# A two-layer graph attention kernel: sums of h behind the first maxima, W's rows on ScalarE's queue, VectorE kept in order at the joint, end stores on other queues

## The chip, the cores and the metric

The kernel runs on one core of one Trainium2 chip. The metric is the device time of one execution in microseconds (us). A profiled execution also gives a span, from its first to its last recorded event, and the clock that was granted to TensorE at each moment.

## What is computed

Two layers are applied to 2708 nodes with 1024 features in float32, over a sparse adjacency matrix. Cut to what matters:

```python
def layer0(x, adj, Wf, bf, Wg, bg, W, bW):
    f, g = x @ Wf + bf, x @ Wg + bg
    e = relu(f @ g.T)
    att = softmax(where(adj > 0, e, NEG), axis=1)
    return att @ (x @ W + bW)

def layer1(x, adj, W, a1, a2):
    h = x @ W
    e = leaky_relu(h @ a1 + (h @ a2).T, 0.2)
    att = softmax(where(adj > 0, e, NEG), axis=1)
    return relu(att @ h)

x = x + layer0(maximum(layernorm(x), 0), ...)
x = x + layer1(maximum(layernorm(x), 0), ...)
```

## The kernel before

**Tiling.** The nodes are cut into five panels of columns (NP = 5; 576, 576, 532, 512 and 512 wide) and ten pairs of row tiles (NQ = 10), with two small tiles left over (MONO and TINY). Every large matrix product is done in seven half-size products, M1 to M7, with sums of blocks before and after (the Strassen-Winograd scheme). The right-hand and left-hand sums of blocks are made by VectorE. Those of h, the normalized rows, lie in DRAM (`hg_d`, seven slots of which `sums_h` fills four, M3 and M5 to M7, from the two that it loads twice: M1 and M2 hold the plain blocks), and are loaded as tiles called `hc` when a product needs them.

**Stages of layer 0**, panel by panel in the loop at L1697: `scores` makes the score tiles S of a panel and accumulates their maxima in `acc`; `project_q(p + 1)` makes the queries of the next panel, and meanwhile, through hooks after its products, `take_max` (M1) turns the maxima by TensorE (`mx_ps`, L849, in `column_max`) and `take_softmax` (M2) makes the exponentials and their sums `sm`; `aggregate` (L885) multiplies S by h in products gx, gy, gz, gv through `accumulate` (L647), whose matmuls are at L661; `inverse_sums` (L858) sums `sm` over partitions with two matmuls into `sum_ps` (L864) and takes reciprocals on VectorE into `rr`; `scale` (L975) multiplies the result gT by them on GpSimd; `project` (L1203, matmuls L1267) multiplies by W and adds the residual x. In panel 0 `aggregate` runs its products in the order M1, M2, M4, M5, M6, M3, M7, in the other panels M1, M5, M2, M6, M3, M7, M4. In the middle of M7, `into_m15` (L933) computes the left-over rows' part (four groups `gw`, L931) and VectorE adds them in.

**The joint.** After the loop, `project(0, 4)` finishes the last panel of layer 0. For each finished row tile, `rows_done` (L1523) normalizes it into `h_last` (ScalarE), takes the dot products with two vectors (`dots(1)`, which the first maxima of layer 1 need, and `dots(0)`, deferred with `put`), and `raise_max` updates `mx`. The last tile calls `shifts1` (L1505), in which `column_max` again turns the maxima (`mx_ps`), and then the column shift m is spread over the partitions by transposes (`sp_ps`, L253) in `weights1` (L1738), which subtracts the spread `mb` from prepared score tiles. Layer 1 then aggregates as layer 0 does and ends with `finish1` (its `go` at L1802), which applies relu, adds the residual and stores to the output.

**W's rows.** `prepare_W` (L1305) loads the rows of the two W (tiles `w_rows`), takes dot products of layer 1's rows with a1 and a2 on VectorE, and makes and stores the sums of W's blocks (`wt_d`).

**What sets the order.** The Tile framework moves instructions within an engine's queue by its own scheduler, unless an instruction is kept in program order; the class `InOrder` does this for the engines named in `nc.hold` (L34 to 54). Loads go through SyncE's queue and are kept in program order (L137); stores go through GpSimd's queue (L141). [...] The tiles `hc`, `hr`, `w_rows`, `hl`, `md`, `As` and `w` share one pool of 12 buffers (`strm`), so a load waits until an earlier tile's last reader is done. Side work is put into a queue `later` (`put`, L198) with a cost in microseconds and, where given, a fetch, which `one` (L201) issues `ahead[0]` items ahead, and a condition `ready`; `behind(us)` (L211) takes items off it between matmuls of a stage, up to the credit of that stage, and `sums_until(n)` and `flush` take them off at once.

Of the kernel before, what the change touches and what calls it, by code (L numbers as in the profile page):

```python
# [12 lines left out]
OP = mybir.AluOpType  # L13
# [5 lines left out]
P = 128  # L19
# [38 lines left out]
def kernel(  # L58
# [152 lines left out]
    def behind(us, psum_free=False):  # L211
# [3 lines left out]
        while spare[0] and not later and lazy and credit[0] > 0:  # L215
            credit[0] -= one(lazy)

    def flush():
        while later:
            one()  # L220
# [141 lines left out]
    def sums_h():  # L362

        def fetch(q, two):
            i, j = group_of[q]
            for m in (M1, M2):
                two.append(stream("hr", (P, 2, W)))
                load(two[-1], hg_d[i][:, m:m + 2, j])

        def first(q, two):  # L370
            (a0, a1), (b0, b1) = ((t[:, 0], t[:, 1]) for t in two)
            add(b1, a1, b1)
            sub(a1, a0, a1)

        def second(q, two):
            (a0, a1), (b0, b1) = ((t[:, 0], t[:, 1]) for t in two)
            sub(a0, b1, a0)
            sub(b0, b0, a0)
            i, j = group_of[q]
            store(hg_d[i][:, M6:M7 + 1, j], two[0])  # L380
            store(hg_d[i][:, M3, j], b0)
            store(hg_d[i][:, M5, j], b1)
            summed[0] += 1
        for q in range(NQ):
            two = []
            put(1.4, lambda q=q, two=two: first(q, two), lambda q=q, two=two: fetch(q, two))
            put(1.4, lambda q=q, two=two: second(q, two))

    BY_QUARTERS = (M1, M5, M2, M6, M7, M3, M4)
    made_quarters = {}  # L390
# [132 lines left out]
            one()  # L523


    def load_rows(w, c, name):
        t = stream(name)
        load(t, w[c * P:(c + 1) * P, :])
        return t

    wgT, wfT, M, m_left = [None, None], {}, {}, {}

# [352 lines left out]
    def aggregate(l, p, S, sm, then={}, rate=3.0):  # L885
# [89 lines left out]
        def scale():  # L975
            for e, s, k in ((0, slice(0, w), w), (1, hi, h)):
                nc.gpsimd.tensor_tensor(of(e, s), of(e, s), by(s, k), OP.mult)  # L977

        accumulate(left, right, NQ, h, order, then, evict, "g",
                   {**prepare, M3: lambda: inverse.append(inverse_sums(p, sm)), M7: scale}, rate=rate,  # L980
                   by_k=True, more={M2: lambda ps: left_over(ps, 0, lo), M3: lambda ps: left_over(ps, 0, hi),
                                    M4: lambda ps: left_over(ps, 1, lo),
                                    (M7, NQ // 2): lambda: (into_m15(), then.get((M7, "middle"), lambda: None)())})
        nc.vector.tensor_tensor(of(1, lo), of(1, lo), by(lo, h), OP.mult)
        return [t.rearrange("p (c i) -> p c i", c=NH) for t in G]

# [318 lines left out]
    def prepare_W():  # L1305
        ab, rows = [], {}

        def fetch(l, k):
            if l == 1 and not ab:
                for k2, a in enumerate((a1, a2)):  # L1310
                    row_to_all(a, wab[k2])
                ab.extend(halves(t) for t in wab)
            rows[l, k] = [load_rows(w_in[l], c, "w_rows") for c in (k, k + NH)]

        def go(l, k):
            two = rows.pop((l, k))
            if l == 1:
                for i, c in enumerate((k, k + NH)):
                    for j in range(2):
                        dot(wa[:, j, c:c + 1], halves(two[i]), ab[j])  # L1320
            right_of_W(l, k, *two)

        for l in range(2):
            for k in range(NH):
                put(2.7 if l == 0 else 8.0, lambda l=l, k=k: go(l, k), lambda l=l, k=k: fetch(l, k))
# [197 lines left out]
    def rows_done(t, xt):  # L1523
# [14 lines left out]
        if panel_of[t] == NP - 1:  # L1538
            done_rows[t] = row_halves("h_last")
            normalize(xt, done_rows[t])  # L1540
            if whole and q == NQ - 1:
                tc.keep_in_program_order(nc.scalar.activation(stats.tile([P, 1], FP, name="warm"), eps, AF.Exp))
            raise_it = lambda: raise_max(0, q, k, first_mask[t][:, :width[0]])
            if not whole:
                dots(1)
                raise_later.append(raise_it)
                put(1.6, lambda: dots(0))
            else:
                raise_later.pop()()
                dots(1)  # L1550
                raise_it()
                put(1.6, lambda: dots(0))
                rest = []
                make = lambda: rest.append(pair_h(q, *(done_rows[s] for s in pairs[q])))
                if q == NQ - 1:
                    got["zm"] = shifts1(0, make)
                else:
                    make()
                rest[0]()
                put_max(1, q)  # L1560
                if q == NQ - 1:
                    for m in BY_QUARTERS:
                        put_quarters(m, q // 2, later)
                    for p in range(2, NP):
                        for s in (NQ - 2, NQ - 1):
                            put_max(p, s, lazy)
            return
# [123 lines left out]
    def take_max(p):  # L1691
        got["m"] = column_max(p, got["acc"])
# [6 lines left out]
    for p in range(NP):  # L1699
# [3 lines left out]
        S = got["S"]  # L1703
        hooks = {M1: lambda p=p: take_max(p), M2: lambda p=p: take_softmax(p)}
        if p == 0:
            hooks[M1] = lambda: (take_max(0), sums_until(3))
            sums_h()
        if p + 1 < NP:
            B = project_q(p + 1, hooks)
        else:  # L1710
# [1 line left out]
            project(0, p - 1, G.pop(p - 1), finish0(p - 1), hooks)  # L1712
            nc.hold = ()
            scores_before()
        then = {M4: lambda: sums_until(NQ), M5: prepare_W} if p == 0 else {}
        ahead[0] = 1 if p == 0 else 2
        if p == NP - 2:
            then[M2] = lambda: first_masks(NP - 1, 0)
# [11 lines left out]
        if p < NP - 2:  # L1730
            project(0, p, G.pop(p), finish0(p), {M1: lambda p=p: first_masks(p + 1, 0),
                                                 M5: lambda p=p: first_masks(p + 1, 1),
                                                 M7: lambda p=p: first_masks(p + 1, 2)})
    flush()
    project(0, NP - 1, G.pop(NP - 1), finish0(NP - 1), by_pair=True, rate=0.0)


    def weights1(p, z, m, shift):  # L1738
# [6 lines left out]
            spread(vb1, columns_of(p, m))  # L1745
        if p == 0:
            mb = slot("mb")
            spread(mb, columns_of(p, shift))
        else:
            spreads()  # L1750
        S = [None] * NT
# [3 lines left out]
        def go(i, mk):  # L1755
            if i < len(order):
                q, k = order[i]
                n, t = P, units[q][k]
                if p == 0 and t in before:
                    S[t] = before.pop(t)  # L1760
                    s = S[t][:n, :w]
                    sub(s, s, mb[:n, :w])
                else:
                    if p == 0 and not spreaded:
                        spreads()
                        spreaded.append(True)
                    S[t] = slot("P")
                    s = S[t][:n, :w]
                    nc.scalar.activation(s, vb1[:n, :w], AF.Identity, bias=f2s[:n, t:t + 1])
                    nc.vector.scalar_tensor_tensor(s, ub[:n, :w], f[1][:n, t:t + 1], s, op0=OP.add, op1=OP.max)  # L1770
                    add(s, s, mk[0][:n, :w])
                nc.scalar.activation(s, s, AF.Exp)
            if i >= LAG:
                q, k = order[i - LAG]
                total(p, sm, S[units[q][k]], once(q, k), i == LAG)
            exps[0] += 1
# [10 lines left out]
    def finish1(p):  # L1787
# [12 lines left out]
                    load(xs[t][e], x1_d[t][:, e * W:(e + 1) * W])  # L1800

        def go(t, e, c):  # L1802
            o = slot("o")[:, :c.shape[1]]
            nc.scalar.activation(o, c, AF.Relu)
            add(xs[t][e], xs[t][e], o)
            if t == TINY:
                for ps, to in by_quarters(out, places[t][0][1], e):
                    store(to, xs[t][e][ps])
# [58 lines left out]
```

## Time and profile before

| | before |
|---|---|
| median of three runs | 3084.98 us (3083.76 to 3087.26) |
| profiled execution, its own time | 3084.88 us |
| span of the profiled execution | 3083.0 us |
| mean granted TensorE clock | 0.991 of full |
| instructions | 41611 |
| TensorE (PE) busy | 3000.3 us, 97% |
| VectorE (DVE) busy | 2069.9 us, 67% |
| GpSimd (POOL) busy | 504.1 us, 16% |
| ScalarE (ACT) busy | 460.9 us, 15% |
| data moved by DMA | 766.79 MB, mean 249 GB/s |

How to read the lines below. In a timeline a line has the start in us, the length in us, the engine (SPq is SyncE's queue of DMA issues), the line of the kernel, the operation, output and inputs, the shape, how many, and in brackets the idle time before it and what ended it. Line 45 is the helper through which VectorE and ScalarE operations are recorded, so there the tile names tell what it is. In the table of waits a line names the engine and its waiting instruction, after the arrow who released it, and then the total, the count and the longest wait in us. In the table of windows a line has the window, its length, the busy time of TensorE's matmuls, its weight loads, VectorE, ScalarE and GpSimd with the number of instructions, then the granted clock, the DMA share and GB/s.

### The profile page before, as it was taken

Reading aid. Unit: us, or ns where it says so; the run is one execution under the profiler, and the core shown is the slowest. Engines: PE = TensorE matmul, PEld = TensorE weight load, DVE = VectorE, ACT = ScalarE, POOL = GpSimd, SP = SyncE. Lnnn points to the kernel's source line nnn. Section 1 sums busy time; section 2 is a strip of 40 time slices with the busy share of each in tenths; the row PEclk is TensorE's granted clock in tenths of the full one; section 3 lists DMA queues with packets and bytes.
Section 4 is the critical chain, followed back from the end, with each engine's and each line's share of the span. In section 5 each row is a group of like instructions: output and inputs, shape, how many; then the busy total and the mean of one; then the engine's idle time right before and its main releaser. Section 6 shows DMA issues by size and latency. Waiting matters only on the chain.

```text
span 3083.0 us, 41611 instructions
## 1 busy us (share of the span) xinstructions
PE 3000.3 (97%) x14630; PEld 2299.3 (75%) x14630; DVE 2069.9 (67%) x4615; ACT 460.9 (15%) x815; POOL 504.1 (16%) x786
## 2 busy tenths in 40 slices
PE   8998999899999999999999999998999999999998
PEld 4576777657877588885888887784767959879695
DVE  5766692776651596716966276867878768887853
ACT  3420020000110101101011001302222131212200
POOL 1421101310011110214102011131202010020202
PEclk9999999999999999999999999998999999999999
DMA  6989967998565796758967588689767768888797
GB/s 226 300 257 272 291 244 255 307 281 226 178 234 154 216 261 223 246 156 239 274 212 249 161 237 272 225 292 327 242 207 254 270 205 293 292 267 295 265 296 248
DMA packets 447808, 766.79 MB, mean 249 GB/s; under 512 B 175488, under 2 KB 262304, under 8 KB 447568
## 3 DMA queue, kind: packets, MB, share of 16 engines
q1 hardware_dynamic: 392624, 598.30, 62.0%
q0 software_dynamic: 54976, 165.83, 16.5%
q8 instruction: 116, 1.90, 0.2%
q14 instruction: 92, 0.75, 0.1%
HBM read 630.04 MB, written 138.11 MB: 249 GB/s over the span
## 4 chain that ended last, share of the span: by engine, by line
PE 74%; DVE 11%; issue 7%; DMA 5%; POOL 1%; SPq 1%; ACT 1%; POOLq 0%; DVEq 0%; ACTq 0%
PE sz L1378 6%; PE gx L661 6%; PE gy L661 6%; PE gz L661 5%; PE gz L1067 5%; PE sx L1378 4%; PE pz L1267 4%; PE px L1267 4%; PE sy L1378 4%; PE py L1267 3%; PE gy L1067 3%; PE gx L1067 3%; PE gv L661 3%; PE M_ps L574 3%; PE qz L661 2%
## 5 line engine op out<-in xcount | busy, mean ns | idle before, releaser
L1378 PE MATMUL sz<-B,As 128*128 128x288 f32 (+2 forms) x1200 | 296.1, 396 | 10.2 <-DVE st L45 8.1
L1378 PEld LDWEIGHTS sz<-B,As 128*128 128x128 f32 x1200 | 229.8, 192 | 61.0 <-DVE st L45 12.1
L1378 PE MATMUL sx<-B,As 128*128 128x288 f32 (+2 forms) x800 | 201.7, 395 | 8.2 <-DMA As<-hs_d 6.2
L1378 PE MATMUL sy<-B,As 128*128 128x288 f32 (+2 forms) x800 | 199.2, 392 | 0.5 <-DMA As<-hs_d 0.5
L661 PE MATMUL gz<-Sa,hc 128*128 128x288 f32 (+2 forms) x800 | 188.3, 396 | 5.9 <-DMA hc<-hg_d 5.9
L1378 PEld LDWEIGHTS sx<-B,As 128*128 128x128 f32 x800 | 152.3, 191 | 42.7 <-issue 5.0
L661 PEld LDWEIGHTS gz<-Sa,hc 128*128 128x128 f32 x800 | 153.3, 192 | 39.2 <-DMA hc<-hg_d 6.3
L1378 PEld LDWEIGHTS sy<-B,As 128*128 128x128 f32 x800 | 152.1, 190 | 31.4 <-issue 0.9
L1067 PE MATMUL gz<-quarter,hc 128*128 128x128 f32 (+2 forms) x1344 | 168.8, 279 | 3.8 <-DVE gT L45 3.7
L143 POOL DMA_DIRECT2D out_dram<-x_res x180 | 88.8, 500 | 482.2 <-DVE x_res L45 471.1
L1067 PEld LDWEIGHTS gz<-quarter,hc 128*128 128x128 f32 x1344 | 160.6, 191 | 5.1 <-DVE gT L45 4.5
L1267 PE MATMUL px<-w,gT 128*128 128x512 f32 x320 | 141.2, 593 | 1.5 <-ACT pt L45 1.5
L1267 PE MATMUL py<-w,ps 128*128 128x512 f32 x320 | 142.2, 593 | 0.0
L1267 PE MATMUL pz<-w,ps 128*128 128x512 f32 x320 | 142.1, 594 | 0.0
L143 POOL DMA_DIRECT2D mk_d<-mask x55 | 35.9, 653 | 530.6 <-DVE mask L45 524.2
L1267 PEld LDWEIGHTS pz<-w,ps 128*128 128x128 f32 x320 | 60.2, 190 | 76.2 <-issue 71.0
L1267 PEld LDWEIGHTS py<-w,ps 128*128 128x128 f32 x320 | 60.5, 190 | 75.1 <-issue 72.7
L1267 PEld LDWEIGHTS px<-w,gT 128*128 128x128 f32 x320 | 60.1, 190 | 72.9 <-issue 67.8
L574 PE MATMUL M_ps<-wgT,wfT 128*128 128x512 f32 x256 | 111.8, 593 | 1.6 <-ACT hsT L45 1.6
L661 PE MATMUL gy<-T,hc 128*128 128x288 f32 (+2 forms) x480 | 111.6, 394 | 0.0
L977 POOL TENSOR_TENSOR gT<-gT,rr 128x2304 f32<-128x2304 f32 (+5 forms) x12 | 44.4, 3698 | 375.6 <-DVE rr L45 172.4
L661 PEld LDWEIGHTS gy<-T,hc 128*128 128x128 f32 x480 | 91.2, 190 | 19.5
(379 smaller groups left out, 5809.6 us busy)
## 6 DMA issues: line engine op xcount, KB each, us to landing
hc<-hg_d SPq DMA_DIRECT2D x175, 512.0 KB
As<-hs_d SPq DMA_DIRECT2D x150, 512.0 KB
hc<-hr_d SPq DMA_DIRECT2D x119, 512.0 KB
hc<-hs_d SPq DMA_DIRECT2D x112, 512.0 KB
w<-wt_d SPq DMA_DIRECT2D x96, 512.0 KB
w<-in_L_gnn_W_dram SPq DMA_DIRECT2D x72, 512.0 KB
md<-md_d SPq DMA_DIRECT2D x56, 512.0 KB
adj_i<-in_adj_dram SPq DMA_DIRECT2D x200, 128.0 KB
```

What stands on the lines that cost most here:

```text
L143: nc.gpsimd.dma_start(a, b)
L574: nc.tensor.matmul(ps, wfT[a][c // NH][:, c % NH, :], wgT[b][c], start=(c == 0), stop=(c == NC - 1))
L661: nc.tensor.matmul(ps[d], left(m, k, d), right(m, k), start=(start and k == 0), stop=(k == K - 1), skip_group_check=True)
L977: nc.gpsimd.tensor_tensor(of(e, s), of(e, s), by(s, k), OP.mult)
L1067: nc.tensor.matmul(ps[:, d], lhs[:, d * P:(d + 1) * P], inner_right(m, n, k), start=(start and k == 0 and d == 0), stop=(k == NK - 1), ski ...
L1267: nc.tensor.matmul(ps, left[i][m][:, k, :], w_[k], start=(start and k == 0), stop=(k == NH - 1), skip_group_check=True)
L1378: nc.tensor.matmul(ps[:n, :h], lefts[q][:, i % 2, c, :n], B[m][c // 2][:, c % 2, :h], start=(start and c == 0), stop=(c == NH - 1), skip_g ...
```

## The change

Six edits:

1. A helper `held` runs a function with VectorE kept in program order.
2. `sums_h`: the fetches of the first two pairs are issued at once, ahead of the loads of the next panel's queries; every item is held in order, and may be taken only after `take_max` has run (`"m" in got`). The hook after M1 of panel 0 no longer calls `sums_until(3)` and runs `take_max` held.
3. `load_rows` gets an argument for the queue. W's rows are loaded by ScalarE's queue, in program order, and `prepare_W` is called after M2 of panel 0's aggregate and no longer after M5, so the first rows are asked for in the third product, M4.
4. `inverse_sums` is called in the middle of M7, ahead of `into_m15`, and no longer at the end of M3, in all five panels of layer 0 and in panel 0 of layer 1.
5. At the joint `project(0, 4)`, `dots(0)`, the spread of `mb` and the first three subtractions of `weights1` are held in order on VectorE.
6. `finish1` of the last panel: relu and addition become one VectorE instruction in place of one on ScalarE and one on VectorE. The last two row tiles are stored by SyncE's and ScalarE's queues in turn, 16 stores, and no longer by GpSimd's.

```diff
+    def held(f, *a):
+        was, nc.hold = nc.hold, ("vector",)
+        r = f(*a)
+        nc.hold = was
+        return r
...
         for q in range(NQ):
             two = []
-            put(1.4, lambda q=q, two=two: first(q, two), lambda q=q, two=two: fetch(q, two))
-            put(1.4, lambda q=q, two=two: second(q, two))
+            if q < 2:
+                fetch(q, two)
+            put(1.4, lambda q=q, two=two: held(first, q, two), None if q < 2 else lambda q=q, two=two: fetch(q, two),
+                ready=lambda: "m" in got)
+            put(1.4, lambda q=q, two=two: held(second, q, two), ready=lambda: "m" in got)
...
-    def load_rows(w, c, name):
+    def load_rows(w, c, name, by=load):
         t = stream(name)
-        load(t, w[c * P:(c + 1) * P, :])
+        by(t, w[c * P:(c + 1) * P, :])
         return t
+
+    def by_scalar(o, i):
+        tc.keep_in_program_order(nc.scalar.dma_start(o, i))
...
         accumulate(left, right, NQ, h, order, then, evict, "g",
-                   {**prepare, M3: lambda: inverse.append(inverse_sums(p, sm)), M7: scale}, rate=rate,
+                   {**prepare, M7: scale}, rate=rate,
                    by_k=True, more={M2: lambda ps: left_over(ps, 0, lo), M3: lambda ps: left_over(ps, 0, hi),
                                     M4: lambda ps: left_over(ps, 1, lo),
-                                    (M7, NQ // 2): lambda: (into_m15(), then.get((M7, "middle"), lambda: None)())})
+                                    (M7, NQ // 2): lambda: (inverse.append(inverse_sums(p, sm)), into_m15(), then.get((M7, "middle"), lambda: None)())})
...
-            rows[l, k] = [load_rows(w_in[l], c, "w_rows") for c in (k, k + NH)]
+            rows[l, k] = [load_rows(w_in[l], c, "w_rows", by_scalar) for c in (k, k + NH)]
...
-                put(1.6, lambda: dots(0))
+                put(1.6, lambda: held(dots, 0))
...
-            hooks[M1] = lambda: (take_max(0), sums_until(3))
+            hooks[M1] = lambda: held(take_max, 0)
             sums_h()
...
-        then = {M4: lambda: sums_until(NQ), M5: prepare_W} if p == 0 else {}
+        then = {M2: prepare_W, M4: lambda: sums_until(NQ)} if p == 0 else {}
...
     flush()
+    nc.hold = ("vector",)
     project(0, NP - 1, G.pop(NP - 1), finish0(NP - 1), by_pair=True, rate=0.0)
+    nc.hold = ()
...
-            spread(mb, columns_of(p, shift))
+            held(spread, mb, columns_of(p, shift))
...
-                    sub(s, s, mb[:n, :w])
+                    (held if i < 3 else lambda f, *a: f(*a))(sub, s, s, mb[:n, :w])
...
         def go(t, e, c):
-            o = slot("o")[:, :c.shape[1]]
-            nc.scalar.activation(o, c, AF.Relu)
-            add(xs[t][e], xs[t][e], o)
+            if p == NP - 1:
+                nc.vector.scalar_tensor_tensor(xs[t][e], c, 0.0, xs[t][e], op0=OP.max, op1=OP.add)
+                if t in full(p)[F // 2:]:
+                    for i, (ps, r) in enumerate(places[t]):
+                        by = nc.scalar if i % 2 else nc.sync
+                        by.dma_start(out[r:r + ps.stop - ps.start, e * W:(e + 1) * W], xs[t][e][ps])
+                    return
+            else:
+                o = slot("o")[:, :c.shape[1]]
+                nc.scalar.activation(o, c, AF.Relu)
+                add(xs[t][e], xs[t][e], o)
```

More of the change, by code (lines that the diff above doesn't have):

```diff
@@ L1551, in rows_done @@
                 raise_it()
-                put(1.6, lambda: dots(0))
+                put(1.6, lambda: held(dots, 0))
                 rest = []
```

## The prediction

> **What bounds the kernel now.** I read the page first (busy shares), then the table of waits of TensorE, then the timelines of the engine that each wait names, and last the clock records beside them. Times below are of the profiled execution: span 3083.0 us, its own time 3084.88 us, so 1.9 us lie around the span; the median of the runs shown, 3084.98 us, is the same to 0.1 us, and what I take off one I take off the other.
>
> ```profile
> PE 3000.3 (97%) x14630; PEld 2299.3 (75%) x14630; DVE 2069.9 (67%) x4615; ACT 460.9 (15%) x815; POOL 504.1 (16%) x786
> ```
>
> TensorE (PE) is the bound, and no matmul of any size is added or removed. Only its idle 83 us can be won, and the time it loses to a lowered clock. Who holds it up is in the waits of TensorE (total, times, longest):
>
> ```profile
> PE mx_ps L849 <- DVE mx L45: 8.3, 1, 8.3
> ...
> PE gz L661 <- DMA hc<-hg_d: 5.9, 1, 5.9
> PE sum_ps L864 <- DVE gT L45: 5.5, 1, 5.5
> PE mx_ps L849 <- DVE acc L45: 5.1, 1, 5.1
> ...
> PE sp_ps L253 <- DVE m L45: 4.4, 2, 3.9
> ```
>
> Five single waits of 3.9 to 8.3 us, 28.6 us together, each in one place; the diff goes to just these places, and to the tail after the last matmul (3072.6 to 3083.0). What such a wait costs besides itself is in the table of windows; the column before the DMA share is the granted clock:
>
> ```profile
> 380.00:400.00 20.00, 14.87 (x55) 11.26 (x55) 13.49 (x24) 2.60 (x6) 3.64 (x6) 0.83 0.98 388
> 530.00:560.00 30.00, 24.13 (x94) 18.41 (x93) 19.23 (x51) 0.00 (x0) 7.70 (x16) 0.89 1.02 410
> 560.00:600.00 40.00, 34.55 (x144) 25.37 (x143) 31.07 (x68) 0.41 (x1) 16.28 (x18) 0.91 0.88 293
> 2120.00:2150.00 30.00, 17.75 (x48) 9.76 (x47) 24.36 (x73) 8.81 (x15) 6.71 (x10) 0.73 0.87 282
> ```
>
> The clock records show it halved for 6.83 us from 389.38, 542.98 and 577.12, and for 17.07 us from 2133.59. Work inside such a stretch takes double, so half of it is lost: TensorE resumes at 391.41 and the stretch ends at 396.21, 4.8 us, 2.4 lost; likewise 546.57 to 549.81, 1.6 lost; 579.99 to 583.95, 2.0 lost; at the joint about 9 us of work, 4.5 lost.
>
> **What the Trainium skill says.** "TensorE: Matmul & The Clock Gate", section "What's actually happening": an idle window of about 3.4 us lowers the clock to half, and a busy one restores it. The trace agrees: the stretches are 3.41, 6.83 and 17.07 us, and follow gaps of 2 us and more. "DMA: Bandwidth & Descriptors", section "Issuing engines are not separate DMA queues": a second issuing engine saves only issue time, since all share the same DMA engines. Here what counts is another thing, the in-order queue of SyncE; the trace of before has no DMA of ScalarE to compare. "SBUF — State Buffer", section "Who interferes with whom": VectorE (DVE) and GpSimd share one port pair under an exclusive lock. The trace agrees: a w_rows addition beside GpSimd's 5.30 us product took 5.42 us instead of 0.69, and a copy out of PSUM beside it 0.68.
>
> **The change, part by part.**
>
> *First maxima (sums_h, take_max).* VectorE at 384 to 392:
>
> ```profile
> 385.34 0.69 DVE L45 TENSOR_TENSOR hr<-hr 128x512 f32<-128x512 f32 x1 [7.09 <-DMA hr<-hg_d]
> ...
> 386.62 0.69 DVE L45 TENSOR_TENSOR hr<-hr 128x512 f32<-128x512 f32 x1
> 387.22 0.75 DVE L45 TENSOR_TENSOR acc<-acc,Sa 128x576 f32<-128x576 f32 x1
> ...
> 390.62 0.74 DVE L45 TENSOR_TENSOR acc<-acc,Sb 20x576 f32<-20x576 f32 x1
> ```
>
> A sum of h stands at the head of VectorE's in-order queue and waits 7.09 us for its DMA; behind it stand the last masks and the accumulation of maxima that mx_ps needs. The chain from 385.34 to the end of 390.62's row is 6 us. With the sums put behind the maxima it starts some 7 us earlier and ends near 384, while TensorE has product M1 of the next panel's queries until 386.28. So the 5.13 us and the 2.4 us of clock go: -7.5. The sums themselves (40 of 0.6 us, 10 of which came before) stand beside 97% TensorE work up to the aggregate's M4; VectorE has some 20 us free there and about 17 us are left to do. The first four hr loads move ahead of the next panel's hT loads on SyncE's queue, 4 x 0.5 us with slack. A hold is added: take_max is kept in order, and hr sums behind it in VectorE's order wait for later hr loads; queued behind them are evictions. I take 0 for this; from below 0, from above 3.
>
> *W's rows by ScalarE.* SyncE's queue before:
>
> ```profile
> 517.46 4.21 SPq L139 DMA_DIRECT2D w_rows<-in_L_gnn_W_dram  x2
> 525.21 0.33 SPq L139 DMA_DIRECT2D hc<-hg_d  x1
> ...
> 534.19 1.05 SPq L139 DMA_DIRECT2D w_rows<-in_L_gnn_W_dram  x2
> 536.25 2.34 SPq L139 DMA_DIRECT2D hc<-hg_d  x4
> ```
>
> A w_rows load waits for a free buffer and holds back the hc loads of the next product; these go out at 536.25, and gz starts at 546.57 after 5.87 us. ScalarE has no work from 483.6 to 590.9, so 16 issues there (no row of before; SyncE's unblocked ones take 0.33 to 0.52 us, 5 to 8 us in all) cost nothing, even when they block. Gain 5.87 + 1.6 = 7.5. Against it: 4 MB of w_rows now come at 484 to 500 with the hc loads of M4, at a DMA share that was 1.02 in 530 to 560. The hc that M4 needs at 495 and 502 I put at landing between 490 and 498 (from 4.5 to 8.3 us that such loads take). Bounds 0 to 3 us of waiting, taken 1.5. Net -6.0.
>
> *inverse_sums to the middle of M7.* Before, sum_ps at the end of M3 needs a PSUM bank that a gT addition has to empty, and that addition is queued behind W's dot products on VectorE (from 574.25 on they run one after another, and the gT rows come at 579.48). In M7's middle the y banks are long empty: 5.45 + 2.0 = -7.5. New: after the two sum_ps, of four gw groups only two find banks, the others wait for the reciprocals, which take 1.9 us (128x288) and 1.7 us (128x256). TensorE has gw0, gw1 and what the order puts between, so 0.3 to 0.5 us stay open per place where VectorE is idle; the bare wait without filler would be 1.4. Six places: 0 to 8.4, taken 2.4. GpSimd's scaling starts later by this; before project needs it, 5 us remain. Net -5.1.
>
> *Joint (project of panel 4, weights of layer 1).* Between 2128.54 and 2136.87 VectorE's chain sets the wait. Off it come a g addition (0.69) and a dot (0.76): -1.45. But in order, the second tile's BN statistics and residual addition, done before while ScalarE normalized the first, stand behind the first tile's two dots: +1. After mx_ps, one g and three to four dots (0.69 each) leave the chain to m: -2.7. The idle total drops from 12.2 to about 9, and the lowered clock by a little: in all -3.5, bounds -1 and -8. The dots come later, in panel 0 of layer 1, where VectorE is full; I see nobody on TensorE waiting for f[0] there before the second panel.
>
> *End.* After the last matmul:
>
> ```profile
> 3072.65 0.69 DVE L45 TENSOR_TENSOR pt<-pv,pt 128x512 f32<-128x512 f32 x1 [1.35 <-PE pv L1267]
> 3073.38 0.63 ACT L45 ACTIVATE o<-pt 128x512 f32<-128x512 f32 x1 [2.81 <-DVE pt L45]
> 3074.04 0.69 DVE L45 TENSOR_TENSOR x_res<-x_res,o 128x512 f32<-128x512 f32 x1 [0.69 <-ACT o L45]
> 3075.02 1.96 POOL L143 DMA_DIRECT2D out_dram<-x_res  x4 [1.48 <-DVE x_res L45]
> ```
>
> One row of the scalar_tensor_tensor kind (0.69 for 128x512) replaces ScalarE's 0.63 and the addition's 0.69, with one handover less: -0.68. The four stores went out one by one, 0.28 + 1.96; two each on two queues take 1.0 to 1.3: -1.0. The rest, 5 us after the last transfer with no row, stays. -1.7, bounds -0.7 and -2.5.
>
> Sum: -7.5 - 6.0 - 5.1 - 3.5 - 1.7 = -23.8; 3084.9 - 23.8 = 3061.1 us.
>
> **The rivals.** (a) As summed, 3061; with my middle terms at both bounds (new waits 0 and joint -8, or twice the new waits and joint -1) 3053 to 3067.5. Chance 0.56. (b) A gap moves: hc for M4 comes late behind w_rows, or an eviction stands behind a sum that waits for its hr load. Then one of the first two gains (7.5) is given back with its half clock: 3061.1 + 7.5 = 3068.6, up to 3072 with some of the reciprocals. For it: the DMA share near 1.0 in those windows; against: the loads are spread, and hc buffers are asked for earlier than before. 0.20. (c) Given back: both gaps move and the joint gains nothing, 3061.1 + 15 + 3.5 = 3079.6; the edits do what they say, only elsewhere something is late by as much; this is within 0.2%. 0.12. (d) Slower: the reciprocals stand behind other VectorE work in each of the six middles of M7. TensorE then waits w for a bank, and from about 2 us on the clock halves too. Without my 2.4 the gain is 26.2; slower by over 0.2% (6.2 us) needs 32.4 us in six places, 5.4 each, about 3.5 of waiting and 1.9 of clock. With w = 4.5: 6 x 6.5 - 26.2 = +12.8, 3097.7. For it: 1.9 us is the dearest VectorE row of this size, and in panels 0, 4 and layer 1's first VectorE is busy; against: in panels 1 to 3 it is idle there (waits of up to 11.0 us for gw). 0.12.
>
> **How the numbers follow.** 0.2% of the time, 6.2 us, is about what a measurement of this kernel tells from no change. Faster is (a) and (b), 0.76; same (c), 0.12; slower (d), 0.12. The range that leaves out (d) and the outer tail of (a) goes from 3053 to 3081; the likeliest time is that of (a), 3061.
>
> **What would show it.** In the profile after: no mx_ps wait on acc and no 7 us wait of hr in front of it; no gz wait on hc near 540; no sum_ps wait on gT; in their place short gw waits on the reciprocals, under 0.6 us each; mx_ps after panel 4 waits 7 to 8 us and sp_ps 1 to 1.5; full clock in 380 to 600; tail 8.7 us instead of 10.4. I am wrong if gx, gy or gv waits for hc in 485 to 510, if gw waits reach 2 us and the clock shows halves in all panels, or if the joint keeps its 12 us.

## The result: slower, and the profile after

The changed kernel takes 3121.19 us (median of four runs, 3116.59 to 3125.15) beside 3085.82 us for the kernel before (3083.76 to 3087.26): a ratio of 1.011, with a 95% interval from 1.0096 to 1.0125. The profiled execution took 3121.07 us with a span of 3119.3 us. The forecast was 3061, faster, with a range up to 3081: it was wrong in sign and in size.

First line of the page after, to be held against that of before (97%, 3000.3 us):

```profile
PE 3017.8 (97%) x14630; PEld 2304.5 (74%) x14630; DVE 2063.6 (66%) x4615; ACT 455.9 (15%) x807; POOL 495.9 (16%) x770
```

TensorE has the same 14630 matmuls and is busy 17.5 us longer. Some 9.6 us of this are matmuls at half clock: its work inside such stretches grows from 34.8 to 54.0 us, and half of the growth is lost. Another 9.9 us are the `gw` matmuls, 26.0 us for 16.1, at an unchanged number of 96 (see inv_only). The two come to 2 us more than the whole, so they are no exact split. Its waits after (total, times, longest):

```profile
PE mx_ps L861 <- DVE mx L45: 9.7, 1, 9.7
...
PE py L1279 <- DMA w<-in_L_gnn_W_dram: 7.1, 1, 7.1
PE gy L673 <- DMA hc<-hg_d: 6.5, 1, 6.5
PE pv L1279 <- DMA w<-wt_d: 6.4, 1, 6.4
PE pz L1279 <- DMA w<-wt_d: 5.8, 1, 5.8
PE gz L673 <- DMA hc<-hr_d: 5.4, 1, 5.4
...
PE px L1279 <- issue: 3.9, 1, 3.9
...
PE gv L673 <- DVE hr L45: 3.4, 1, 3.4
...
PE sp_ps L259 <- DVE m L45: 1.8, 1, 1.8
```

Of the five waits that the forecast wanted gone, those of mx_ps on acc, of gz at 540 and of sum_ps are gone, and that of sp_ps is shorter (1.8 for 3.9). That of mx_ps at the joint is longer, 9.7 for 8.3. Seven new or longer ones of 3.4 to 7.1 us stand here, and five of them name a DMA. The windows show where the clock fell (the column before the DMA share):

```profile
380.00:400.00 20.00, 20.00 (x89) 15.62 (x88) 18.39 (x36) 5.10 (x10) 5.09 (x9) 1.00 0.60 195
...
485.00:525.00 40.00, 31.38 (x114) 22.88 (x113) 23.95 (x56) 0.00 (x0) 10.85 (x20) 0.87 1.03 417
530.00:560.00 30.00, 30.00 (x126) 23.49 (x125) 17.79 (x53) 0.00 (x0) 3.25 (x6) 1.00 0.88 329
560.00:600.00 40.00, 40.00 (x168) 29.46 (x167) 8.48 (x12) 0.00 (x0) 4.42 (x4) 1.00 0.70 196
2120.00:2150.00 30.00, 18.45 (x51) 9.61 (x50) 22.96 (x62) 7.83 (x13) 7.22 (x11) 0.73 0.74 245
...
3070.00:3119.00 49.00, 24.25 (x40) 9.27 (x38) 6.65 (x10) 0.00 (x0) 0.00 (x0) 0.77 0.33 107
```

The windows 380 to 400 and 530 to 600, at 0.83 to 0.91 before, are whole and at full clock now. New holes are 485 to 525, which was busy throughout and at full clock before, and the end. Since the order of matmuls is nearly the same in both kernels, I set each matmul's start in the one profile against its start in the other. The difference (after minus before) moves like this; the times are those of before, and all numbers are in us:

| stretch | difference grows by | what lies there |
|---|---|---|
| start to 290 | +1.3 | nothing of the change: start-up |
| 290 to 402 | -7.7 | first maxima without a wait |
| 402 to 483 | +5.8 | hl (the left-over rows of h) late (2.0), gv after hr (3.4), half clock |
| 483 to 525 | +14.9 | hc late in M4 and at M5 (1.8, 6.5), half clock twice |
| 525 to 605 | -13.7 | waits of gz and sum_ps gone |
| 605 to 700 | -2.5 | a wait of 2.2 at 677 of before is absent, as it is in end_all_act, which has no edit there |
| 700 to 2060 | +5.0 | steps of 1.4 to 1.7 in each of panels 1 to 3, no wait shown |
| 2060 to 2168 | -2.0 | the joint, with what led up to it |
| 2168 to 2229 | +8.1 | gz waits for hc (5.4), half clock |
| 2229 to 2315 | +5.3 | M7's middle, then px (3.9 for 1.5) |
| 2315 to last matmul | +27.3 | three waits for w, half clock after each |
| tail | -5.5 | 4.9 us for 10.4 |

The sum is +36.3, the difference of the two spans. Such a table says where, not why, and two of its lines could have the same cause. That is what the runs are for.

### The profile page after: what moved, and what is told of

Read it like the earlier page. It is cut to its first block, busy times and chain, and to the rows that moved or that the text cites. A ratio compares the mean times of both kernels' runs of the same rounds, so it can differ in the third digit from the quotient of the medians.

```text
span 3119.3 us, 41647 instructions
## 1 busy us (share of the span) xinstructions
PE 3017.8 (97%) x14630; PEld 2304.5 (74%) x14630; DVE 2063.6 (66%) x4615; ACT 455.9 (15%) x807; POOL 495.9 (16%) x770
## 3 DMA queue, kind: packets, MB, share of 16 engines
q0 software_dynamic: 54464, 164.78, 16.1%
## 4 chain that ended last, share of the span: by engine, by line
PE 72%; issue 11%; DVE 10%; DMA 5%; POOL 1%; ACT 1%; SPq 1%; POOLq 0%; DVEq 0%; ACTq 0%
PE gz L673 7%; PE gy L673 7%; PE gz L1079 5%; PE sz L1390 5%; PE gx L673 5%; PE pz L1279 4%; PE py L1279 4%; PE px L1279 4%; PE sy L1390 3%; PE M_ps L586 3%; PE sx L1390 3%; PE gx L1079 3%; PE gy L1079 3%; PE gv L673 3%; PE qz L673 3%
## 5 line engine op out<-in xcount | busy, mean ns | idle before, releaser
L1390 PE MATMUL sx<-B,As 128*128 128x288 f32 (+2 forms) x800 | 203.1, 397 | 12.8 <-DMA As<-hs_d 11.5
L143 POOL DMA_DIRECT2D out_dram<-x_res x164 | 81.2, 502 | 467.1 <-DVE x_res L45 456.8
L673 PEld LDWEIGHTS gy<-T,hc 128*128 128x128 f32 x480 | 92.9, 194 | 27.3 <-issue 6.9
```

The source lines that it names most:

```text
L143: nc.gpsimd.dma_start(a, b)
L673: nc.tensor.matmul(ps[d], left(m, k, d), right(m, k), start=(start and k == 0), stop=(k == K - 1), skip_group_check=True)
L1390: nc.tensor.matmul(ps[:n, :h], lefts[q][:, i % 2, c, :n], B[m][c // 2][:, c % 2, :h], start=(start and c == 0), stop=(c == NH - 1), skip_g ...
```

## The experiments

Ratios are to the kernel before in runs beside it. Between executions the first 290 us of the program differ by up to 10 us in the profiles below (waits for As at 230 to 290), so I go by ratios with their intervals for the size, and by the waits in a profile for the place.

**The end alone (end_only).** The diff's last hunk (`go` in `finish1`), and nothing else.

> The kernel before with the edit of the end alone. Theory: the output stores on SyncE's queue wait for x_res and hold back the loads of W that stand behind them in the same in-order queue, so TensorE waits three times for w (5.8, 7.1 and 6.4 us in the changed kernel, and the lowered clock after each), and the tail after the last matmul is 5.5 us shorter: about 3085 + 27 - 5.5 = 3107 us. Rival: the waits for w at the end come from something that is delayed upstream, in layer 1; then this edit alone is worth -1 to -5 us, 3080 to 3084.

Measured: 3112.67 us, ratio 1.0087 (1.007 to 1.0104). This is the theory's side, and some 5 us more than its 3107; the profile has the same three waits (5.8, 8.3 and 6.5 us). SyncE's queue in the changed kernel shows how:

```profile
3074.00 0.81 SPq L1822 DMA_DIRECT2D out_dram<-x_res  x2
3074.91 1.83 SPq L139 DMA_DIRECT2D w<-wt_d  x4
3090.99 0.80 SPq L1822 DMA_DIRECT2D out_dram<-x_res  x2
3091.90 0.93 SPq L139 DMA_DIRECT2D w<-in_L_gnn_W_dram  x2
3103.13 0.81 SPq L1822 DMA_DIRECT2D out_dram<-x_res  x2
3104.03 0.86 SPq L139 DMA_DIRECT2D w<-wt_d  x2
```

Every load of w goes out within 0.1 us after a pair of stores, and the stores go out when VectorE has made x_res. TensorE waits for that w, VectorE can make the next x_res only after that, and the next store waits for this x_res. A store on the queue of loads so ties the prefetch of w to the output of the half tile before. Before, the last loads of w went out at 3050.14.

**The same stores on ScalarE's queue (after_end_act, end_all_act).** In the changed kernel:

```diff
-                        by = nc.scalar if i % 2 else nc.sync
+                        by = nc.sync if i % 2 and t == full(p)[-1] and e == 1 else nc.scalar
```

> The changed kernel with the end's 16 stores on ScalarE's queue, which has nothing else to do there; of the very last half tile two of the four stay on SyncE's. Theory (stores block the loads of W behind them): the three waits for w go and the short tail stays, 3121 - 27 = 3094 us. Rival (the waits come from upstream): about 3118 to 3121.

Measured: 3103.71 us, ratio 1.0059 (1.0044 to 1.0074), where the theory had 3094. Two of the three waits are gone; the one left (py for w, 8.0 us at 3077) is at the one half tile that kept two stores on SyncE's queue, which was not the last one to be finished. So in the kernel before, the end's edit with no store on SyncE's queue:

```diff
-                        by = nc.scalar if i % 2 else nc.sync
-                        by.dma_start(out[...], xs[t][e][ps])
+                        nc.scalar.dma_start(out[...], xs[t][e][ps])
```

> The kernel before with the edit of the end, but all 16 stores on ScalarE's queue and none on SyncE's. Theory: with no store ahead of a load of W, none of the three waits for w is left (the one left in after_end_act was at a store on SyncE's queue), and the tail after the last matmul is about 5 us instead of 10.4: 3088 - 5 = 3083 us. Rival: ScalarE's queue, blocked by waiting stores, delays its copies of px, so TensorE waits and the gain is lost: 3088 or more.

Measured: 3082.35 us, ratio 0.9982 (0.9975 to 0.999): a gain of 4 to 6 us, and none of the three waits. VectorE at its end:

```profile
3077.39 0.69 DVE L45 TENSOR_TENSOR pt<-pv,pt 128x512 f32<-128x512 f32 x1 [2.02 <-PE pv L1267]
3078.11 0.69 DVE L45 SCALAR_TENSOR_TENSOR x_res<-pt,x_res 128x512 f32<-128x512 f32 x1
```

The fused row takes the place of ScalarE's relu and the addition; from its end, 3078.80, to the end of the span, 3082.84, are 4.0 us, where it was 8.3 before (3074.73 to 3083.03). The two single waits of before, on ScalarE and for GpSimd's issue, cost less than the rest of the tail (see the last section).

**The sums of h alone (sums_only).** The hunks in `sums_h` and the hook of M1, with `held`.

> The kernel before with the sums of h put behind the first maxima, and nothing else. Theory: the wait of mx_ps on acc goes (-7.7), but the sums, now later and held in order on VectorE, wait for their hr loads in M1 and M2 of the aggregate and hold back the differences of the fourth step that product M4 needs, so gv waits 3 to 4 us and the clock falls: about 3081 to 3084 us. Rival: those waits in M2 and M4 come from W's rows that use the DMA engines at the same time; then they are absent here and it ends at 3085 - 7.7 = 3077 us.

Measured: 3086.03 us, ratio 1.0003 (0.9994 to 1.0012). The wait of mx_ps is gone and 7.7 us with it (the difference to before falls from -1.6 at 290 to -9.3 at 402), and by 483 it is back at -3.2 and at 684 at -2.9: TensorE waits 2.5 us for hl at 467 and runs at half clock for 6.83 us from 471. The theory's place was right, its detail not: here the late tile is hl, not VectorE's differences. The hl load stands on SyncE's queue behind the hr loads, and these wait for buffers that are free only when earlier sums have been stored; in the changed kernel, the table of SyncE's waits from 470 to 525 has at its head

```profile
SPq L139 <- DMA hg_d<-hr: 23.9, 3, 10.0
SPq L139 <- DMA wt_d<-w_rows: 22.3, 5, 7.1
```

that is, queue time spent on the stores of sums and of W's sums. In sums_only itself SyncE's queue waits 17.8 us for such stores from 440 to 475. Since the rival (no waits without W's rows) would have given 3077, it falls.

**Only the first fetches early (sums_early_fetch).** The sums themselves stay ahead of the maxima:

```diff
+            if q < 2:
+                fetch(q, two)
-            put(1.4, lambda q=q, two=two: first(q, two), lambda q=q, two=two: fetch(q, two))
+            put(1.4, lambda q=q, two=two: first(q, two), None if q < 2 else lambda q=q, two=two: fetch(q, two))
```

> The kernel before with only the first two fetches of hr put ahead of the loads of the next panel's queries; the sums stay where they were, ahead of the first maxima, and are not held. Theory: the 7 us of VectorE's wait at 378 to 385 was only for these loads, so the wait of mx_ps on acc (5 to 6 us, and 2.4 of clock) goes, and hl at 467 is not late, because the other sums and their loads keep their old times: 3088 - 7.5 = 3081 us. Rival: the third pair's load, which is not early, makes VectorE wait in its turn, and the gain is below 2 us.

Measured: 3087.96 us, ratio 1.0003 (0.9994 to 1.0011). The theory falls: VectorE waits 7.08 us at 373 to 380 for hr as before, only earlier, and then again for the third pair:

```profile
390.43 0.69 DVE L45 TENSOR_TENSOR hr<-hr 128x512 f32<-128x512 f32 x1 [2.74 <-DMA hr<-hg_d]
```

**W's rows alone (w_only).** The hunks of `load_rows`, `prepare_W` and its place (`then`).

> The kernel before with W's rows loaded by ScalarE's queue and asked for from the third product on, and nothing else. Theory: the late hc of before at 540 is gone (-7.5), and sum_ps no longer waits long on gT, since W's dots end earlier on VectorE (another -5 to -7.5); but W's rows load the DMA engines while hc for M4 and M5 is fetched, and the products before 520 wait for hc 6 to 9 us with the half clock after it: 3085 - 14 + 12 = 3083 us. Rival: the waits for hc at 497 and 510 in the changed kernel came from the sums of h that sat on the same buffers and on SyncE's queue; then they are absent here: 3072 to 3075 us.

Measured: 3081.47 us, ratio 0.9979 (0.9971 to 0.9986). Both waits, at 540 and at 575, are gone, though inverse_sums was not moved; and hc and hl are late in M4 (3.0 us at 491, 6.5 at 500, 14.3 us with the clock). ScalarE's queue and then SyncE's show it:

```profile
480.16 54.42 ACTq L45 DMA_DIRECT2D w_rows<-in_L_gnn_W_dram  x16
```

```profile
485.98 0.32 SPq L139 DMA_DIRECT2D hc<-hg_d  x1
489.38 6.29 SPq L139 DMA_DIRECT2D wab<-in_L_gnn_a_dram  x2
495.84 0.38 SPq L139 DMA_DIRECT2D hl<-hgl_d  x1
498.71 19.45 SPq L139 DMA_DIRECT2D hc<-hg_d  x7
```

Eight of the sixteen w_rows went out between 480.2 and 485.4, one after another. In the stretch 478 to 512 SyncE's queue waited 28.2 us for buffers in which w_rows were still being loaded and 12.8 us for stores of W's sums. hl, needed at 500, went out at 495.84. The DMA engines were full too (share 0.97 in 480 to 510), so two runs tell the causes apart.

**Buffers of their own for W's rows (w_own_10_2).** As w_only, and:

```diff
-    strm = ctx.enter_context(tc.tile_pool(name="strm", bufs=12))
+    strm = ctx.enter_context(tc.tile_pool(name="strm", bufs=10))
+    wrows = ctx.enter_context(tc.tile_pool(name="wrows", bufs=2))
...
-        t = stream(name)
+        t = wrows.tile([P, D], FP, tag="wr", name=name) if name == "w_rows" else stream(name)
```

> As w_only, but W's rows have two buffers of their own and the other streamed tiles ten in place of twelve. Theory: in w_only ScalarE issued eight w_rows loads within 5 us of 480 and so took the free buffers of the shared pool; the loads of hc and hl for M4 stood on SyncE's queue waiting for the W tiles to be stored, and that made the waits of 3.0 and 6.5 us at 491 and 500. With own buffers these waits fall under 2 us together and the gains at 540 and 575 stay: 3088 - 14 + 3 = 3077 us. Rival: the waits come from the DMA engines, which are full from 482 to 508 (share 0.9 to 1.0); with two buffers W's loads still come early, so part of the waits stays, and ten buffers cost elsewhere: 3082 to 3088 us.

Measured: 3106.68 us, ratio 1.0062 (1.0043 to 1.008). Between 402 and 524 no hc or hl is late, and TensorE's waits there come to 0.5 us: that part of the theory holds. But with two buffers W's rows come so slowly that VectorE stands at them, up to 8.8 us at a time, while the additions that empty the gv of M4 are due behind (gap of 16.8 us at 524). In the scores As is late by 2.0 and 2.4 us (at 1143 and 1877), which costs about 4 us each with the clock; that this is due to ten buffers in place of twelve is likely, as best1 has such a wait too, and not tested alone. As a kernel it is a miss.

**Early, but on SyncE's queue (w_sync_early).** One line:

```diff
-        then = {M4: lambda: sums_until(NQ), M5: prepare_W} if p == 0 else {}
+        then = {M2: prepare_W, M4: lambda: sums_until(NQ)} if p == 0 else {}
```

> The kernel before with W's rows begun in the third product, but still on SyncE's queue, in line with the loads of hc. Theory: what made TensorE wait at 491 and 500 in w_only is that ScalarE's queue ran ahead of the products and took eight buffers at once; in SyncE's queue each w_rows load stands behind the hc loads of its own product, so hc is not late in M4, and the waits at 540 and 575 shrink because W is done earlier: 3087 - 10 = 3077 us. Rival: the waits at 491 and 500 come with the early start itself (DMA engines full, buffers short), whichever queue: as w_only, 3080, or, because a blocked w_rows load then holds back the hc loads behind it, 3085 to 3095 us.

Measured: 3077.65 us, ratio 0.9969 (0.9958 to 0.998), the lowest ratio of a single edit, though its interval touches that of w_only. The waits in M4, first in w_only and then here:

```profile
PE gv L930 <- DMA hl<-hgl_d: 6.5, 1, 6.5
...
PE gv L664 <- DMA hc<-hg_d: 3.0, 1, 3.0
```

```profile
PE gv L927 <- DMA hl<-hgl_d: 2.9, 1, 2.9
PE gv L661 <- DMA hc<-hg_d: 2.5, 1, 2.5
```

The profiles of the two combinations below repeat this: 6.5 and 3.0 with ScalarE's queue (w_end), 1.1 and 3.4 with SyncE's (w_sync_early_end). So about half of those waits comes from ScalarE's queue that runs ahead, and the other half stays with the early start; what makes that half stays open. Full DMA engines don't make the difference between the two: their share in 480 to 510 is 1.02 here, for 0.97. With the clock the stretch costs 10.8 and 8.1 us on SyncE's queue, for 14.3. What the change's other queue was to bring, it has without it.

**inverse_sums alone (inv_only).** The hunk of `aggregate`.

> The kernel before with inverse_sums moved to the middle of M7 in all six places, and nothing else. Theory: panel 0 gains 7.5 (the wait of sum_ps on gT and its half clock), but in every one of the six the left-over groups gw, short of banks, are taken apart, and TensorE needs about 1.6 us more for the same matmuls without showing a wait (9.6), and px at the start of layer 1's projection waits 2.4 us longer: 3085 - 7.5 + 12 = 3089.5 us. Rival: the regrouping costs nothing and the drift of 1.3 to 2.5 us per panel comes from elsewhere: 3085 - 7.5 = 3077.5 us.

Measured: 3096.41 us, ratio 1.0033 (1.0019 to 1.0046): more than the theory's 3089.5, and on its side. The four groups `gw` of M7 were in one piece before, and are apart now. TensorE in panel 1 before, and in the changed kernel:

```profile
961.44 1.13 PE L864 MATMUL sum_ps<-sm,ones 128*128 128x288 f32 x4
962.41 11.80 PE L661 MATMUL gz<-Sa,hc 128*128 128x288 f32 x48
974.05 2.10 PE L927 MATMUL gw<-Sa,hl 128*128 128x288 f32 x8
976.09 0.77 PE L931 MATMUL gw<-Sb,hl 20*128 20x288 f32 x8
976.78 8.03 PE L661 MATMUL gz<-Sa,hc 128*128 128x288 f32 x32
```

```profile
972.14 1.13 PE L939 MATMUL gw<-Sa,hl 128*128 128x288 f32 x4
973.20 0.75 PE L943 MATMUL gw<-Sb,hl 20*128 20x288 f32 x4
973.88 0.75 PE L939 MATMUL gw<-Sa,hl 128*128 128x288 f32 x2
974.57 0.75 PE L943 MATMUL gw<-Sb,hl 20*128 20x288 f32 x2
975.24 1.24 PE L673 MATMUL gz<-Sa,hc 128*128 128x288 f32 x4
976.32 0.65 PE L939 MATMUL gw<-Sa,hl 128*128 128x288 f32 x2
976.90 0.75 PE L943 MATMUL gw<-Sb,hl 20*128 20x288 f32 x2
```

The groups gw take 2.73 us in one piece before (974.05 to 976.78), and 3.10 + 1.25 = 4.35 in three pieces after: eight matmuls of 20 rows need 0.77 us together, but two need 0.75 as well. No wait is shown; the 1.6 us are in the matmuls' own rows. Over the six places all `gw` take 26.0 us here as in the changed kernel, for 16.1 before. These 9.9 us, with px at the start of layer 1's projection (4.0 us for 1.5, and its clock), are more than the move gains in panel 0, where the stretch 525 to 605 brings -4.6. Between 700 and 1790 the difference to before changes by at most 0.4 us in eleven profiles without this edit (the two with ten buffers left out, where loads are late), and grows by 4.8 to 5.1 in the three with it. Why the scheduler took the groups apart is argued and not shown: the kernel holds TensorE's results in a pool of eight buffers, its banks, sum_ps keeps two of them until the reciprocals, and the order fills that time.

**inverse_sums behind gw (inv_after_gw).**

```diff
-                                    (M7, NQ // 2): lambda: (into_m15(), then.get((M7, "middle"), lambda: None)())})
+                                    (M7, NQ // 2): lambda: (into_m15(), then.get((M7, "middle"), lambda: None)(), inverse.append(inverse_sums(p, sm)))})
```

> The kernel before with inverse_sums in the middle of M7, but behind the left-over groups gw in place of ahead of them. Theory: what cost 1.6 us in each of six places was that the four gw groups were taken apart because two of the banks were held by sum_ps until the reciprocals; behind gw, the groups stay together and the cost falls to under 0.5 us each, while the wait of sum_ps on gT in panel 0 is gone all the same: 3085 - 7.5 + 2 = 3079.5 us. Rival: the cost is that of sum_ps or the reciprocals standing in M7 at all, wherever in it: 3088 to 3096 as in inv_only.

Measured: 3096.14 us, ratio 1.0023 (1.0015 to 1.0031). The groups stay together (`gw` 16.1 us again) and the drift from panel 1 to 4 falls to about 0.4 us each, as the theory said. The total does not fall: projection now waits 2.1 us at 602, 4.0 at 647 and 8.2 at 2310 (px for 1.5 before). The reciprocals are later still, and with them GpSimd's scaling of gT, which in panel 0 ends at 601.2, 2.7 us before px starts (603.90). So both explanations have a share: the grouping is shown by the `gw` times, the late rr by the order in the timeline alone.

**The joint alone (joint_only), and with free dots (joint_free_dots).** The hunks of `rows_done`, the last `project` and `weights1`; then the same without `held` around `dots`.

> The kernel before with the joint's edit alone: dots(0), project(0,4), the spread of mb and three subtractions held in order on VectorE. Theory: the dots that before ran in the gaps of the joint are put off into panel 0 of layer 1, where VectorE is full; there they delay the raising of the maxima, so the mask loads (maskl) on SyncE's queue wait longer for buffers and the hc loads behind them come late: gz waits about 5 us at 2220, and the half clock adds 2 to 3. The joint itself gains 2 to 3.5. In sum 3085 - 3 + 8 = 3090 us. Rival: the gz wait comes from another edit (the end of the scores or the reciprocals), and this one alone gains: 3082 us.

> As joint_only, but dots(0) is not held in order, so VectorE may take these dot products where it has a hole, as in the kernel before. Theory (the put-off dots delay the masks and so hc): the gz wait at 2220 is under 2 us as before, and the joint keeps a part of its gain: 3083 to 3085 us. Rival (the wait has another origin, such as the held subtractions): the same time as joint_only, 3088 to 3091.

Measured: 3093.4 us, ratio 1.0018 (1.0009 to 1.0026), and 3091.26 us, ratio 1.0004 (0.9993 to 1.0016). The two intervals overlap, so the waits, one profile each, have to tell them apart. With the dots held, gz waits 5.1 us at 2224 and the clock is half for 6.83 us; with the dots free that wait is gone. The chain: in the stretch 2190 to 2232 SyncE's queue waited for VectorE's maxima, before and then with the held dots (joint_only),

```profile
SPq L139 <- DVE mx L45: 1.1, 2, 0.7
```

```profile
SPq L139 <- DVE mx L45: 13.2, 2, 12.8
```

The late maxima hold the buffers of the masks, the mask loads stand on SyncE's queue, and hc, as well as the sums of hq, come late behind them. The joint itself has 9.7 + 1.8 us of waiting (mx_ps and sp_ps) with the dots held and 10.2 + 3.3 with the dots free, for 8.3 + 3.9 before. So the gain with the dots held is 0.7 us of waiting, with them free there is none, and the theory's second half (a part of the gain stays) fails. The little that the joint gains hangs on putting the dots off, and putting them off is what costs.

**Combinations.** best1 takes w_own_10_2, sums_early_fetch and end_all_act together:

> Three parts together: W's rows by ScalarE's queue with two buffers of their own, the first two hr fetches early, and the end with all its stores on ScalarE's queue; no edit of the joint and none of inverse_sums. If each is worth what it should be alone (11, 7.5 and 5 us): 3088 - 23 = 3065 us. If the gains of the first two exclude each other because DMA or buffers are short: 3072 to 3078 us.

Measured: 3101.64 us, ratio 1.005 (1.0035 to 1.0065); as bad as its first part, with the gap of 16.7 us at 523, and 13.7 at 584 on top. Then w_only and end_all_act (w_end), and the changed kernel without the move of inverse_sums and with end_all_act's stores (after_no_inv):

> W's rows on ScalarE's queue (w_only, which measured 6.5 us less than before) together with the end whose stores are all on ScalarE's queue (end_all_act, 5 us less), nothing else. The two places are 2500 us apart and share nothing, so the gains should add: 3087 - 11.5 = 3075 us. If they don't, one of the two was a difference of start-up between executions: 3080 to 3083 us.

> The changed kernel with the end's stores all on ScalarE's queue and with inverse_sums at the end of M3 as before. Theory: with W's rows early the wait of sum_ps on gT is gone without the move, so the move only costs (six times 1.6 us of TensorE for gw taken apart, 2.4 at px): from after_end_act's 3104, less about 10 for the last wait for w with its clock, less 12: 3082 us. Rival: the move is still needed, because the dots of W behind the sums of h end late: sum_ps waits 5 us and more at 575 again, 3089 us or above.

Measured: w_end 3076.15 us, ratio 0.9966 (0.9958 to 0.9974): the two gains nearly add up (0.9979 and 0.9982 make 0.9961). after_no_inv 3081.47 us, ratio 0.9988 (0.9979 to 0.9997): sum_ps does not wait at 575, so with W's rows early the move was needless, and between 700 and 2060 the difference to before now grows by 0.4 us in place of 5.0. Last, w_sync_early with end_all_act:

> The version that the runs point to: W's rows begun in the third product but on SyncE's queue (0.31% less than before), and the end with all its stores on ScalarE's queue (0.14 to 0.18% less), no other edit. If the two add, a ratio of 0.9953, 3072 us beside a before of 3086.6; if the short waits at 491 and 500 in M4 were short by luck in one group of runs, 0.997, as w_end.

Measured: 3074.57 us, ratio 0.9952 (0.9939 to 0.9966). Two small edits of the whole change, both in another form, beat both kernels. Its interval and that of w_end overlap, so that SyncE's queue is better than ScalarE's here is likely and not proved.

**Added up.** Place by place the single edits give nearly all of the changed kernel's table: from 290 to 402 sums_only has -7.7; from 402 to 525 sums_only and w_only have +6.1 and +14.3, for +20.7; from 525 to 605 w_only has -15.4 and one place of `gw` +1.7, for -13.7; from 700 to 2060 inv_only has +6.1, for +5.0; from 2168 to 2229 joint_only has +8.1, for +8.1; from 2229 to 2315 inv_only has +6.5, for +5.3; and from 2315 to the last matmul end_only has +30.7, for +27.3. No large part of the loss needs two edits together.

## Why the prediction was wrong, step by step

**The end** failed most: forecast -1.7, measured +27.3 for TensorE and -5.5 for the tail. The step priced the stores at what they take to issue ("two each on two queues take 1.0 to 1.3") and did not ask what is queued behind them. The working of W's rows, on SyncE's queue at 534, had the very mechanism: a transfer that waits holds back the loads behind it. The tail itself was under-priced: 4.9 to 5.5 us and not 1.7, and in end_all_act it is the whole gain. The step held that the 5 us after the last transfer stay; they fell to 1.4 in the changed kernel.

**First maxima**: the gain was right (-7.5 forecast, -7.7 measured). The cost of the moved sums was put at 0, "from above 3"; it measured 6 to 7 us with its half clock (sums_only), because VectorE's time was counted, but not the place of the hr loads on SyncE's queue ahead of hl.

**W's rows**: the gain was right at 540. The new waits were put at 1.5 with a bound of 3, and came to 9.5 us and some 5 of clock in w_only. I had weighed the DMA engines' share and landing times, and took the buffers to be "asked for earlier than before"; but ScalarE has nothing to wait for and took eight buffers of the pool of twelve within 5.3 us. That the 16 issues cost nothing was right for ScalarE and wrong for the pool.

**inverse_sums**: the 7.5 us were counted for this edit, but the wait of sum_ps on gT was made by W's dots on VectorE, as the step itself said; W's rows earlier take it away alone (w_only, after_no_inv). So the sum counted it once where it should, but the price of the edit bought nothing. The price, 0.3 to 0.5 us a place, was 1.6 without any visible wait: I had looked for TensorE waiting for the reciprocals, and the scheduler filled that time in a way that made the matmuls dearer. Rival (d), six places that sum up, named an edit that does cost, but not the dearest one and not by its mechanism, and its threshold of 5.4 us a place was far from reached. That the kernel did get slower is no success of it.

**Joint**: -3.5 forecast; in the four profiles with the dots held the stretch 2100 to 2168 brings -0.6 to -1.7, and profiles without the edit vary there from +0.3 to -1.0, so hardly a gain is shown. The wait of sp_ps fell by 2.1 us, for 2.7 forecast. That of mx_ps was to fall to 7 to 8 us and rose from 8.3 to 9.7. The second tile's dots did come 1 us later after the first tile's, as the step had it (5.77 us for 4.71), and the rows taken off saved 1.0 in place of 1.45. A further 1.3 us was in no term: the first tile's dots started with TensorE's last matmul before (2128.53 and 2128.54), and 1.3 us after it now (2132.65 and 2131.35). Then the dots' new place failed: "I see nobody on TensorE waiting for f[0] there". Nobody waits for f[0]; masks' buffers wait for the maxima behind the dots, and hc waits behind the masks. 8.1 us in the changed kernel, ratio 1.0018 alone.

Rival (b), one gap that moves, was the right kind: three moved, not one, and the end was in no rival. Two of the signs that the prediction set for itself came: gv waits 1.8 us for hc at 497 (and gy 6.5 at 510), and the joint keeps 11.5 of its 12.2 us. One small reading in it is off: the copy of 0.68 us that it sets beside GpSimd's product of 5.30 ran beside the next one, of 2.61 us.

The new waits lowered the clock as the page that the prediction cites lets expect (the Trainium skill, "TensorE: Matmul & The Clock Gate", section "What's actually happening"): six of the seven brought 6.83 us of half clock each, and px 3.41. Here a shorter gap than the page's idle window of about 3.4 us did it too: the 2.5 us for hl in sums_only were followed by 6.83 us. The prediction also cited that a second issuing engine saves only issue time ("DMA: Bandwidth & Descriptors", section "Issuing engines are not separate DMA queues") and set this aside for the in-order queue. The runs agree with the page as far as they go: w_sync_early has the gain of W's rows without ScalarE's queue.

## What to carry to other kernels

Before moving a DMA to another queue, list what stands behind it there and what it waits for: a store that waits for a result must not share an in-order queue with loads that feed that result's successors. A queue with nothing to wait for runs ahead and takes shared buffers from the one that must keep pace. And work put off from a gap into an engine that is full comes back as a buffer that is free too late, often two queues away.

## What the runs showed of the hardware that was not expected

The end of the program after the last transfer depends on the queue of the last stores. With GpSimd's queue, 5.0 us lay between the end of the last transfer (3078.0) and the end of the span (3083.03), and also in inv_only. With ScalarE's queue (end_all_act) it was 1.3 us (3081.5 to 3082.84), and in four more profiles with the last stores on SyncE's and ScalarE's queues 1.3 to 1.4. These 3.7 us are most of the tail's gain.

A short run of matmuls costs more than its share of a long one. Of the 20-row matmuls eight in a row took 0.77 us and two took 0.75; of the 128-row ones eight took 2.10 and two 0.65 to 0.75. Taking one set of groups apart cost 1.6 us with no wait in the profile, and 9.9 us in six places.
